# Softmax sums in one row of 512, added tile by tile, and query projections spread over more half steps

## The chip, the cores and the metric

The kernel runs on one core of a Trainium2 chip. A core has engines that work side by side, each through its own queue in order: PE (TensorE, matrix products and transposes), DVE (VectorE), ACT (ScalarE), POOL (GpSimd) and SP, which here only issues DMA transfers. The metric is the device time of one execution in microseconds (us); less is better. PE writes its results to PSUM, in banks of 128 partitions by 512 float32 numbers; the other engines read them from there.

## The reference

A decoder of two layers works on x of shape (4, 256, 256), that is four sequences b of 256 tokens. Layer 0 has self-attention, attention to a context of 1601 tokens, and a feed-forward part with ternary weights. Layer 1 has a gated recurrence, attention to the same context with projections, and a mixture of eight experts. The change touches the attention of layer 1, which is, cut to what matters:

```python
q = rms_norm((draft @ Wq.T).reshape(b, 256, 16, 128), q_norm_w)       # 16 query heads of 128
kv_in = concatenate([context, draft], axis=1)                         # 1857 keys
k = rms_norm((kv_in @ Wk.T).reshape(b, 1857, 4, 128), k_norm_w)       # 4 key heads
v = (kv_in @ Wv.T).reshape(b, 1857, 4, 128)
q, k = rope(q, draft_positions), rope(k, all_positions)
scores = einsum('bhqd,bhkd->bhqk', q, repeat(k, 4)) / sqrt(128)
attn = einsum('bhqk,bhkd->bhqd', softmax(scores), repeat(v, 4))
out = attn.reshape(b, 256, 2048) @ Wo.T
```

The softmax runs over the keys. The change alters how the sums of the exponentials, its denominators, are added up, and when the queries are projected.

## The kernel before

Layer 0 and the recurrence fill the first 450 us or so. Then comes a long stage of 32 *pairs*: for each b and each key head g (together a *head* in the code, 16 of them, list `heads`) two pairs of query heads. A pair (class `Pair`) has 512 columns, two query heads of 256 tokens, and 15 key chunks of 128 keys, handled as 8 tiles of two chunks (the last tile holds one chunk of 65 keys). Keys lie on partitions, queries along the row, so a tile is 128 x 2 x 512.

A pair passes through these methods:

- `score` (L1169): for each chunk PE makes the scores into a PSUM bank (bsc, L1181), ACT copies them with the factor of the keys (kn) into an s tile (L1182), and DVE keeps the running maximum (acc, L1184 and L1186). The s tiles come from a ring of 12 (`s_tile`, `NS`), so that the tile of step t is written again in step t + 12.
- `maximum` (L1188): PE transposes acc (tm), DVE reduces it, and PE spreads the maxima over a bank (bc, L1199).
- `exponential` (L1201): DVE subtracts bc from the s tile (L1203), ACT takes the exponential in place (L1206), and POOL adds the tile to `sum` (L1209 for tiles 0 and 1, L1211 for the rest). `sum` has 2 x 512 columns in one buffer.
- `weigh` (L1213): PE multiplies the values with the exponentials (bpo, L1220).
- `finish` (L1222): POOL adds the two halves of `sum` (L1225), ACT copies bpo out (aT, L1228), PE transposes the sum (ts, L1232), DVE reduces and inverts it (rs), PE spreads it (rb, L1239), DVE scales aT, and after the second pair of a head PE projects the result (bpw, L1247).

The next head is prepared meanwhile. `prep_q` (L1068 on; two calls a head, j = 0 and 1) projects 128 tokens onto four query heads (pq, L1078). In `rotate` ACT squares the result (L1033) and DVE makes two products (ropeq L1034, ropuq L1035). In `factor` POOL adds the halves of the rotation (L1040), DVE sums the squares (L1042), and POOL raises them to the power -1/2 (rnq, L1043). A half step or more later `normed` scales on ACT, four instructions (L1047), and later again PE transposes (tpq, L1090) and ACT copies out (L1091). `prep_kv` (L1097 on; four calls a head) does the same for up to four chunks of keys and values (pk L1115, ropek, ropuk, kn), with the key transposes tpk (L1124) and their copy kTb on ACT (L1126) as its second part. The weights of a head come by DMA on SP's queue (wq, wkv, wo, and context tiles cTk).

The order is written out by hand in `steps` (L1334): step s does the exponential of tile s - 10, the scores of tile s, then the other work of place 2s, the weighing of tile s - 11, then that of place 2s + 1. A place is thus half a step; a pair takes 16 places, a head 32. The loop from L1299 puts the parts of the next head at places: `QA` and `KA` give the steps of the projections of queries and keys after the head's base, `HB` the places from a query projection to its scaling, and `HC` those from a projection to its transposes, for queries and keys alike (L1318). Work that takes a PSUM bank gets a place of its own (`bank=True`): where the place is taken it moves to the next. A scheduler then fixes each engine's queue from this program, and may shift instructions a little where nothing depends on their order.

Short-lived results share six PSUM banks (`p1`): scores, pq, pk, all transposes but bc.

Of the kernel before, what the change touches and what calls it, by code (L numbers as in the profile page):

```python
# [10 lines left out]
F32 = mybir.dt.float32  # L11
# [5 lines left out]
ALU = mybir.AluOpType  # L17
# [3 lines left out]
P = 128  # L21
# [88 lines left out]
def decoder_kernel(ctx: ExitStack, tc: tile.TileContext, at, t, out):  # L110
    nc = tc.nc
    V, A, G, T = nc.vector, nc.scalar, nc.gpsimd, nc.tensor
# [6 lines left out]
    fr = ctx.enter_context(tc.tile_pool(name="fr", bufs=1))  # L119
# [11 lines left out]
    def p1(name):  # L131

        ring[0] += 1
        if psb and ring[0] % 3 == 0:
            return psb[0].tile([P, 512], F32, tag="one", name=name, bufs=2)
        return psa.tile([P, 512], F32, tag="one", name=name, bufs=4)
# [17 lines left out]
    def fa(b, name, dt=F32):  # L154

        return fr.tile([P, 512], dt, tag=f"a{b}", name=name, bufs=NA)
# [9 lines left out]
    def sm(shape, tag, name, bufs=2, dt=F32):  # L166
        return small.tile(shape, dt, tag=tag, name=name, bufs=bufs)
# [18 lines left out]
    def cc(name):  # L186
        o, n = at[name]
        return cst[:, o : o + n]

    ident = cc("ident")  # L190
# [969 lines left out]
    class Pair:  # L1160
# [40 lines left out]
        def exponential(self, c):  # L1201
            n, w, s = self.rows[c], self.wide[c], self.s[c]
            V.tensor_tensor(  # L1203
                s[0:n, 0:w, :], s[0:n, 0:w, :], self.bc[0:n, None, :].to_broadcast([n, w, 512]), ALU.subtract
            )
            A.activation(s[0:n, 0:w, :], s[0:n, 0:w, :], AF.Exp)  # L1206
            if c == 1:
                self.sum = fr.tile([P, 2, 512], F32, tag="sum", name=f"sum{self.nm}")
                G.tensor_tensor(self.sum, self.s[0], s, ALU.add)  # L1209
            elif c > 1:  # L1210
                G.tensor_tensor(self.sum[0:n, 0:w, :], self.sum[0:n, 0:w, :], s[0:n, 0:w, :], ALU.add)  # L1211

        def weigh(self, c):  # L1213
            e = gt[self.b, self.g]
# [7 lines left out]
        def finish(self):  # L1222
            b, g, nm = self.b, self.g, self.nm
            e, su = gt[b, g], self.sum
            G.tensor_tensor(su[:, 0, :], su[:, 0, :], su[:, 1, :], ALU.add)  # L1225
            aT = fa(1, f"aT{nm}")
            e[self.h] = aT
            A.copy(aT, self.po)  # L1228
            yield
            ts = p1(f"ts{nm}")  # L1230
            for i in range(4):
                T.transpose(ts[:, i * P : (i + 1) * P], su[:, 0, i * P : (i + 1) * P], ident)  # L1232
            rs = sm([P, 4], "rs", f"rs{nm}")
            V.tensor_reduce(rs, ts.rearrange("p (i k) -> p i k", i=4), AX.X, ALU.add)
            V.reciprocal(rs, rs)
            yield
            rb = p1(f"rb{nm}")
            for i in range(4):
                T.transpose(rb[:, i * P : (i + 1) * P], rs[:, i : i + 1].to_broadcast([P, P]), ident)  # L1239
            V.tensor_mul(aT, aT, rb)  # L1240
            yield
            if self.h == 2:
                pw = p1(f"bpw{b}{g}")
                for j in range(2):
                    for h in range(4):
                        o = (h % 2) * 256 + j * P
                        T.matmul(  # L1247
                            pw[:, j * 256 : j * 256 + 256], lhsT=e[h - h % 2][:, o : o + P], rhs=e["wo"][:, h, :],
                            start=h == 0, stop=h == 3,
                        )  # L1250
                xf = xs[b].rearrange("p j d -> p (j d)")
                V.tensor_add(xf, xf, pw)
# [6 lines left out]

    QA, KA, HB, HC = (3, 7), (11, 13, 15, 17), 4, 7
    DE, DW = 10, 11
    places, taken = {}, set()
    STEPS = NPAIR * len(pairs) + DW + 5
# [202 lines left out]
```

## Time and profile before

| what | value |
|---|---|
| median of 3 runs | 1853.54 us (1852.35 to 1856.31) |
| the profiled execution: its time, its span | 1854.56 us, 1852.8 us |
| granted TensorE clock, mean | 0.97 |
| PE busy | 1733.6 us (94%) |
| DVE, ACT, POOL busy | 1292.5, 1005.3, 834.9 us |
| POOL adds of exponentials (L1209, L1211, L1225) | 80.4, 424.1, 41.0 us |
| chain that ended last | PE 63%, DVE 11%, POOL 10%, ACT 10%, issue 4% |

The profile is one execution; its span runs from the first to the last instruction. Each line of a group names a source line, engine and operation, the result and the operands, their shape and the count, then busy time, the mean of one, and the time that the engine stood idle just before, with what ended that idleness after the arrow. A line of the waits reads: who, waited for whom: us in total, times, longest. A line of the timeline has the start, the duration, engine, line and operation; in brackets the idle time before it. Some PE records have 128x512 products in two pieces, so that two products count four.

### The profile page before, as it was taken

The page shows a single profiled execution, that of the slowest core. Times are in us where ns is not written, and L with a number is a line of the kernel's source. Part 1 is how long each engine was busy: PE and PEld are TensorE (multiplying, and loading weights), DVE is VectorE, ACT ScalarE, POOL GpSimd, SP SyncE. Part 2 cuts the span into 40 slices and gives each one's busy share as a digit, 9 for nine tenths or more (in the row PEclk, how much of TensorE's full clock was granted, in tenths as well). Part 3 has the DMA queues.
Part 4 walks back from the last instruction along what each step waited for, and adds up shares of the span by engine and source line. Part 5 has one row for each costly group of instructions (what it writes and reads, how often), then busy time and mean ns, then how long its engine had stood idle before and what let it go on. Part 6 is the DMA issues. An engine that isn't in the chain of part 4 may idle for free.

```text
span 1852.8 us, 19989 instructions
## 1 busy us (share of the span) xinstructions
PE 1733.6 (94%) x6576; PEld 1056.6 (57%) x6576; DVE 1292.5 (70%) x2396; ACT 1005.3 (54%) x1898; POOL 834.9 (45%) x524
## 2 busy tenths in 40 slices
PE   4779899989999999999999989999999999999997
PEld 3556786655555554655555555556565655556555
DVE  5785547787777668776767776676868676667754
ACT  1556536464656555665655565555646565455541
POOL 2100332111156565545656555655455566655470
PEclk8789899999999999999999999999999999999998
DMA  4010232001110110101011112101120111112000
GB/s 138 1 40 15 78 113 66 25 24 44 47 54 15 52 37 29 54 21 57 13 59 44 51 37 62 44 29 47 36 83 29 48 44 52 32 35 60 29 23 23
DMA packets 66214, 82.99 MB, mean 45 GB/s; under 512 B 6460, under 2 KB 49600, under 8 KB 66112
## 3 DMA queue, kind: packets, MB, share of 16 engines
q1 hardware_dynamic: 64960, 80.31, 14.2%
q10 hardware_dynamic: 1152, 1.41, 0.2%
q8 instruction: 53, 0.87, 0.2%
q14 instruction: 49, 0.40, 0.1%
HBM read 80.65 MB, written 1.05 MB: 44 GB/s over the span
## 4 chain that ended last, share of the span: by engine, by line
PE 63%; DVE 11%; POOL 10%; ACT 10%; issue 4%; DMA 0%; ACTq 0%; POOLq 0%; DVEq 0%
PE bpo L1220 14%; PE bsc L1181 14%; PE pk L1115 9%; POOL sum L1211 4%; POOL sum L1209 3%; PE bpw L1247 3%; ACT s L1182 3%; ACT s L1206 3%; DVE acc L1186 2%; PE mph L914 2%; PE xpo L607 2%; PE xsc L562 2%; PE pq L1078 1%; PE mpe L925 1%; ACT sm L463 1%
## 5 line engine op out<-in xcount | busy, mean ns | idle before, releaser
L1186 DVE SCALAR_TENSOR_TENSOR acc<-bsc,kn,acc 128x512 f32<-128x512 f32 x448 | 335.0, 748 | 215.9 <-ACT s L1182 205.2
L1181 PE MATMUL bsc<-qTb,kTb 128*128 128x512 f32 (+1 forms) x960 | 455.6, 594 | 5.7 <-DVE acc L1186 3.4
L1220 PE MATMUL bpo<-s,vb 128*128 128x512 f32 (+1 forms) x960 | 455.4, 595 | 1.1 <-ACT aT L1228 1.1
L1211 POOL TENSOR_TENSOR sum<-sum,s 128x1024 f32<-128x1024 f32 x192 | 424.1, 2209 | 16.5 <-ACT s L1206 2.4
L1182 ACT ACTIVATE s<-bsc,kn 128x512 f32<-128x512 f32 (+1 forms) x480 | 316.0, 687 | 184.8 <-PE bsc L1181 111.0
L1203 DVE TENSOR_TENSOR s<-s,bc 128x1024 f32<-128x1024 f32 (+1 forms) x256 | 288.7, 1144 | 13.7 <-PE bc L1199 13.7
L1206 ACT ACTIVATE s<-s 128x1024 f32<-128x1024 f32 (+1 forms) x256 | 254.4, 1013 | 61.2 <-DVE s L1203 59.9
L1220 PEld LDWEIGHTS bpo<-s,vb 128*128 128x128 f32 (+1 forms) x960 | 178.5, 191 | 166.6 <-issue 157.0
L1040 POOL TENSOR_TENSOR ropek<-ropek,ropuk 128x512 f32<-128x512 f32 (+1 forms) x64 | 76.8, 1200 | 402.2 <-DVE ropuk L1035 402.2
L1181 PEld LDWEIGHTS bsc<-qTb,kTb 128*128 128x128 f32 (+1 forms) x960 | 167.5, 187 | 150.4 <-issue 114.1
L1115 PE MATMUL pk<-wkv,cTk 128*128 128x256 f32 x832 | 194.4, 383 | 15.8 <-DVE acc L1186 15.8
L1115 PEld LDWEIGHTS pk<-wkv,cTk 128*128 128x128 f32 x832 | 157.7, 191 | 56.4 <-DVE acc L1186 21.3
L1040 POOL TENSOR_TENSOR ropeq<-ropeq,ropuq 128x512 f32<-128x512 f32 x32 | 41.0, 1282 | 173.0 <-DVE ropuq L1035 125.9
L1209 POOL TENSOR_TENSOR sum<-s,s 128x1024 f32<-128x1024 f32 x32 | 80.4, 2511 | 39.7 <-PE ts L1232 24.9
L1033 ACT ACTIVATE squares<-pk 128x256 f32<-128x256 f32 (+1 forms) x128 | 47.7, 375 | 90.4 <-PE pk L1115 80.8
L1047 ACT ACTIVATE ropeq<-ropeq,rnq 128x128 f32<-128x128 f32 x128 | 44.5, 396 | 91.0 <-POOL rnq L1043 91.0
L1034 DVE TENSOR_TENSOR ropek<-pk,ctabk 128x256 f32<-128x256 f32 (+1 forms) x128 | 52.0, 406 | 56.1 <-ACT squares L1033 55.9
L1118 ACT COPY vb<-pk 128x256 f32<-128x256 f32 (+1 forms) x128 | 46.1, 361 | 65.4 <-DVE ropuk L1035 62.7
L463 ACT ACTIVATE sm<-sc,mx 128x128 f32<-128x128 f32 (+1 forms) x128 | 52.2, 436 | 26.8 <-DVE mx L456 19.9
L1043 POOL TENSOR_TENSOR kn<-ssk,nhalf 128x4 f32<-128x4 f32 (+1 forms) x64 | 63.6, 994 | 0.0
L914 PE MATMUL mph<-yTm,wi 128*128 128x256 f32 x256 | 63.1, 392 | 0.0
L1126 ACT COPY kTb<-tpk 128x512 f32<-128x512 f32 (+1 forms) x64 | 35.2, 550 | 49.8 <-PE tpk L1124 49.8
(494 smaller groups left out, 2530.6 us busy)
## 6 DMA issues: line engine op xcount, KB each, us to landing
cTk<-in_ctxT SPq DMA_DIRECT2D x32, 512.0 KB, 3.8
wq<-in_wq SPq DMA_DIRECT2D x16, 512.0 KB, 4.9
wo<-in_wo SPq DMA_DIRECT2D x16, 512.0 KB, 3.8
wi<-in_wi SPq DMA_DIRECT2D x32, 256.0 KB, 2.9
xcT<-in_ctxT SPq DMA_DIRECT2D x12, 512.0 KB, 3.7
xct<-in_ctx SPq DMA_DIRECT2D x12, 512.0 KB, 3.6
cTk<-in_ctxT SPq DMA_DIRECT2D x16, 384.0 KB, 3.2
wkv<-in_wkv SPq DMA_DIRECT2D x16, 256.0 KB, 3.6
```

The lines of the kernel that those rows point to most:

```text
L463: A.activation(ex[:, h, k], scs[u][:, h, k], AF.Exp, bias=mx[:, j, i : i + 1], accum_out=sums[:, j, i : i + 1])
L914: T.matmul(ph[:, i * 256 : i * 256 + 256], lhsT=wi[:, i, c, f * ME : (f + 1) * ME], rhs=yT[:, c, :], start=c == 0, stop=c == 1,)
L1040: G.tensor_tensor(r4, r4, u4[:, :, ::-1, :], ALU.add)
L1115: T.matmul(pk[:, q, :], lhsT=src, rhs=e["wkv"][:, c, :], start=c == 0, stop=c == 1)
L1181: T.matmul(pc[0:n, :], lhsT=e["kT"][:, k * P : k * P + n], rhs=q, start=True, stop=True)
L1182: A.activation(s[0:n, i, :], pc[0:n, :], AF.Copy, scale=e["kn"][0:n, k : k + 1])
L1186: V.scalar_tensor_tensor(self.acc[0:n, :], pc[0:n, :], e["kn"][0:n, k : k + 1], self.acc[0:n, :], ALU.mult, ALU.max)
L1203: V.tensor_tensor(s[0:n, 0:w, :], s[0:n, 0:w, :], self.bc[0:n, None, :].to_broadcast([n, w, 512]), ALU.subtract)
L1206: A.activation(s[0:n, 0:w, :], s[0:n, 0:w, :], AF.Exp)
L1209: G.tensor_tensor(self.sum, self.s[0], s, ALU.add)
L1211: G.tensor_tensor(self.sum[0:n, 0:w, :], self.sum[0:n, 0:w, :], s[0:n, 0:w, :], ALU.add)
L1220: T.matmul(self.po, lhsT=e["v"][0:n, k, :], rhs=self.s[c][0:n, i, :], start=k == 0, stop=k == NCH - 1)
```

## The change

The sum of a pair becomes one row of 512 columns per partition, in two buffers that take turns between pairs. The first add comes with tile 0 and adds its two halves; each later tile is added half by half, two instructions for a tile of two chunks and one for the last. The add of the two halves at the end is dropped. The projections of queries move from steps 3 and 7 to steps 2 and 6 of the head before; the distance from projection to scaling grows from 4 to 5 places, that to the transposes from 7 to 8, for queries and keys.

```diff
@@ exponential
             A.activation(s[0:n, 0:w, :], s[0:n, 0:w, :], AF.Exp)
-            if c == 1:
-                self.sum = fr.tile([P, 2, 512], F32, tag="sum", name=f"sum{self.nm}")
-                G.tensor_tensor(self.sum, self.s[0], s, ALU.add)
-            elif c > 1:
-                G.tensor_tensor(self.sum[0:n, 0:w, :], self.sum[0:n, 0:w, :], s[0:n, 0:w, :], ALU.add)
+            if c == 0:
+                self.sum = fr.tile([P, 512], F32, tag="sum", name=f"sum{self.nm}", bufs=2)
+                G.tensor_tensor(self.sum, s[:, 0, :], s[:, 1, :], ALU.add)
+            else:
+                for i in range(w):
+                    G.tensor_tensor(self.sum[0:n, :], self.sum[0:n, :], s[0:n, i, :], ALU.add)
@@ finish
-            G.tensor_tensor(su[:, 0, :], su[:, 0, :], su[:, 1, :], ALU.add)
...
-                T.transpose(ts[:, i * P : (i + 1) * P], su[:, 0, i * P : (i + 1) * P], ident)
+                T.transpose(ts[:, i * P : (i + 1) * P], su[:, i * P : (i + 1) * P], ident)
@@ places
-    QA, KA, HB, HC = (3, 7), (11, 13, 15, 17), 4, 7
+    QA, KA, HB, HC = (2, 6), (11, 13, 15, 17), 5, 8
```

## The prediction

> **What bounds the kernel now.** I read the busy shares first, then the idle gaps of PE by what ended them, then the waits of the other engines, then the timeline around the repeated gaps.
>
> ```profile
> PE 1733.6 (94%) x6576; PEld 1056.6 (57%) x6576; DVE 1292.5 (70%) x2396; ACT 1005.3 (54%) x1898; POOL 834.9 (45%) x524
> ```
>
> PE is the bound. The table by stage gives 1320 us of PE work in the 1350 us from 450 to 1800, where the attention pairs run. Only idle PE time there can be won. The waits of PE in that stretch sum to 29.6 us; its three largest are:
>
> ```profile
> PE pk L1115 <- DVE acc L1186: 15.8, 13, 3.2
> PE mpe L925 <- DVE acc L1186: 3.8, 3, 1.3
> PE bsc L1181 <- DVE acc L1186: 3.4, 2, 2.8
> ```
>
> PE waits for a PSUM bank that the running maximum (acc) has yet to read. Why acc is late stands in the waits of all engines:
>
> ```profile
> DVE acc L1186 <- ACT s L1182: 205.2, 118, 5.8
> ACT ropeq L1047 <- POOL rnq L1043: 91.0, 25, 6.3
> ACT s L1182 <- POOL sum L1209: 62.3, 30, 5.5
> POOL sum L1209 <- PE ts L1232: 24.9, 5, 14.0
> ```
>
> acc waits for the score copy on ACT, and ACT waits on POOL: for the first add of a pair (L1209), which is the last reader of an s buffer that ACT wants to refill, and for the norm factors of the queries (rnq). The timeline shows one such case whole:
>
> ```profile
> 832.07 1.28 POOL L1040 TENSOR_TENSOR ropek<-ropek,ropuk 128x512 f32<-128x512 f32 x1 [14.29 <-DVE ropuk L1035]
> 833.30 1.03 POOL L1043 TENSOR_TENSOR kn<-ssk,nhalf 128x4 f32<-128x4 f32 x1
> 834.29 2.43 POOL L1209 TENSOR_TENSOR sum<-s,s 128x1024 f32<-128x1024 f32 x1
> 836.75 1.27 ACT L1182 ACTIVATE s<-bsc,kn 128x512 f32<-128x512 f32 x2 [2.01 <-POOL sum L1209]
> 837.48 0.75 DVE L1186 SCALAR_TENSOR_TENSOR acc<-bsc,kn,acc 128x512 f32<-128x512 f32 x1 [2.09 <-ACT s L1182]
> 838.28 0.48 PE L1115 MATMUL pk<-wkv,cTk 128*128 128x256 f32 x1 [2.40 <-DVE acc L1186]
> ```
>
> POOL stood idle for 14.29 us in front of the key rotation while finished exponentials lay waiting; the first add was queued behind it. The 2.40 us reach PE.
>
> I sort PE's gaps from 510 to 1780 (26.8 us) by what the chain shows before each. (A) First add behind a key rotation: 2.39, 2.40, 1.98, 1.99, 1.97 = 10.7. (B) First add behind a query rotation: 2.76, 0.95, 1.27, 1.26, 1.26 = 7.5. (C) The second query's factor behind the whole sum, and small rest: 8.6.
>
> [...]
>
> **The change part by part.** (1) The adds. Prices from the groups by form:
>
> ```profile
> L1211 POOL TENSOR_TENSOR sum<-sum,s 128x1024 f32<-128x1024 f32 x160 | 382.6, 2391 | 14.1 <-ACT s L1206 2.4
> L1209 POOL TENSOR_TENSOR sum<-s,s 128x1024 f32<-128x1024 f32 x32 | 80.4, 2511 | 39.7 <-PE ts L1232 24.9 <-ACT s L1206 14.9
> L1225 POOL TENSOR_TENSOR sum<-sum 128x512 f32<-128x512 f32 x32 | 41.0, 1280 | 2.5
> L1211 POOL TENSOR_TENSOR sum<-sum,s 65x512 f32<-65x512 f32 x32 | 41.5, 1296 | 2.4
> ```
>
> Before, a pair is 8 adds: 2.42 + 5 x 2.36 + 1.26 + 1.27 = 16.75 us at the medians, and 0.07 after each that the next one needs (the chain's "issue"): 17.3. After, it is 14 adds of 1.27: 18.7. So 1.4 us a pair, 45 us of POOL work more. [...] The 45 us lie beside PE, since POOL is idle 40% of most stages. The cover is missing only in the last pair, where POOL is the chain from 1788.65 to 1805.93. There the first add can start at the end of exponential 0 (1787.4) instead of 1: 1787.4 + 18.7 = 1806.1. Cost: +0.2.
>
> (2) The start of the sum. The first add needs one exponential instead of two, and writes the other sum buffer, so the 24.9 us of POOL waiting for the transposes (ts) fall away. The order of instructions on POOL changes with it: in the pair that starts a head, the first add and most often eight more now precede the key rotation; in the other pair, two or three precede the query rotation. Nothing then holds up the first release: A and B go, -18.2.
>
> (3) The query projections come two half steps earlier (QA), their scaling one (HB), their transposes one (HC). Each brings its wq load, square, two products, sum of squares, rotation and power along, unchanged in number. wq is issued one head ahead on SP's queue (489.65 for the matmul at 547.13) and keeps its place among the loads, so it can't be late. The second factor still follows the whole sum on POOL. The sum starts about 3 us sooner and takes 1.4 longer, so ACT's wait for it shrinks: I credit half of C, -4.3.
>
> (4) HC also serves the keys (KA), which do not move: their four transposes a head come a half step later, while the scores that read them stay. This is the costly part. I counted PE work between the last key transpose and the first score that reads it, in the order of instructions, at 0.86 us a 512-column matmul and 0.216 a 256-column one. Before: 6.1 to 7.0, 5.3 to 6.1, 5.3 to 6.1 and 4.0 to 4.9 us for the four groups. After: 1.0 to 1.4, 3.6, 1.8 to 2.7 and 2.3. In between ACT must copy the keys out (0.43 to 0.59). The trace of before shows how late that copy runs:
>
> ```profile
> 880.13 0.49 PE L1124 MATMUL tpk<-cst,ropek 128*128 128x128 f32 x3
> 881.69 1.27 ACT L1182 ACTIVATE s<-bsc,kn 128x512 f32<-128x512 f32 x2 [3.93 <-POOL sum L1209]
> 882.84 0.43 ACT L1126 COPY kTb<-tpk 128x321 f32<-128x321 f32 x1
> 899.69 0.69 ACT L1047 ACTIVATE ropeq<-ropeq,rnq 128x128 f32<-128x128 f32 x2 [4.06 <-POOL rnq L1043]
> ```
>
> The fourth copy ended 2.65 us after its transposes here, 2.1 to 4.3 over the heads; 2.0 are left after the change. What made it late, the first add, goes, but another wait comes: ACT's scaling of the first query now stands before that copy, and its factor follows three or four adds on POOL. Queued behind the scaling on ACT are two score copies for four times, three exponentials and the key copy; DVE waits for the score copies, PE for their banks and for the keys.
>
> I worked one head through from the start of its bc transposes with the durations above. Exponentials 0 to 2 end at 3.1, 4.7, 6.8; POOL adds to 8.7, rotates to 10.0, adds the other half of tile 2 to 11.2, and the factor is there at 12.2. ACT arrives at 8.5 and loses 3.7. Scaling, two exponentials and four score copies later the fourth key copy ends at 18.4. PE wants it at 16.7: 1.8 us lost. Eight of the 14 later heads have an add between rotation and factor, as this one. Where none is between (six heads) the factor is there at 9.8; four lose nothing and two about 0.85. Sum: 8 x 1.8 + 1.7 = +16.1. Bounds: 0, if ACT runs ahead once the first add no longer stops it, and 15 x 2.7 = 40, if every head loses the 1.8 and the third copy (1.8 us left, copies ended 1.1 to 2.5 late) about 0.9 more. I take 16 since both waits are worked from measured durations. The first group's 1.0 suffices as long as ACT is idle there, as before (it waited 0.8 to 1.9 us for tpk).
>
> Sum: -18.2 - 4.3 + 16.1 + 0.2 = -6.2. The profiled execution took 1854.56 (span 1852.8), 1.02 over the median of the runs: 1848.4, and 1847.4 as a median.
>
> **Rivals.** *Margins hold* (0.20): the new stalls stay under 0.3 us a head, so 22.5 less about 3: 1834. For it: the first factor of a head was waited for 1.7 to 3.2 us before in 8 heads, and in 7 not at all. Against: 2.0 us left where 2.1 to 4.3 were used. *Key copies decide* (0.31), the other side: ACT reaches the fourth, and the third, key copy late in all heads, 2.7 us a head: 40 - 22 = +18, 1871. It decides from 22.5/15 = 1.5 us a head on. For it: in-order ACT, shortened distances in all 15 heads. Against: PE that stalls gives ACT time, so stalls don't add up. *No effect* (0.09): the gaps only move, since PE is 98% full there: 1853.5. For it: 30 waits of 62.3 us for L1209 cost PE only 18. *Mine* (0.40), with its own range 1841 to 1854.
>
> **How the numbers follow.** A measurement tells 0.2% (3.7 us) from no change. Mine is 0.7 faster, 0.25 same, 0.05 slower; margins hold is faster; key copies slower; no effect same. Faster 0.28 + 0.20 = 0.48; same 0.10 + 0.08 = 0.18 (0.01 of no effect given to slower); slower 0.34. The range, with 1 in 10 outside each end, cuts half of "margins hold" and a third of "key copies": 1833 to 1871.
>
> **What would show it.** Right: no ACT wait for a first add and no POOL wait for ts; POOL about 880 us busy in 714 to 720 instructions; new PE or PEld waits of 1 to 2 us ended by kTb before the score matmuls, at most one or two a head; ACT waiting for rnq ahead of the fourth key copy. PE idle from 450 to 1800 near 24 us. Wrong: waits for kTb absent (then 1834), or over 1.5 us in every head (then 1871). A PE gap behind adds that now delay the key rotations would be a mechanism that I have not counted.

## The result, and the profile after

The changed kernel takes 1841.28 us (median of 6 runs, 1837.06 to 1841.77), the kernel before, on the same chip, 1853.36 us (6 runs, 1852.33 to 1856.31). The ratio is 0.9928, with a 95% interval of 0.9917 to 0.9938: 12.1 us faster, where 6 were forecast. The time lies inside the prediction's range, and just inside that of its likeliest case.

The busy time of the engines, from the page of the changed kernel:

```profile
PE 1727.6 (94%) x6576; PEld 1051.1 (57%) x6576; DVE 1288.4 (70%) x2396; ACT 1007.2 (55%) x1896; POOL 871.8 (47%) x716
```

The profiled execution took 1839.59 us, its span is 1837.7 us, 15.1 less than before. PE busy fell by 6.0 us (1733.6 to 1727.6), though the work on PE is the same, and the rest of the span, in which PE stands still, by 9.1 us (119.2 to 110.1). Both are needed for the sum; the prediction counted only the second kind. Nearly all of the gain lies between the first and the last score product (L1181), the *pair stage* from here on: 1300.3 us before and 1285.7 after, with 27.4 and 17.9 us of PE's idle time. What comes ahead of it, the same work in both, took 474.3 and 473.1 us, a difference of the size that these profiles show from one kernel to another (472.3 to 474.8 in all 14).

What PE waited for from 450 to 1800, the view in which the kernel before had "pk <- acc" with 15.8 us at its head:

```profile
PE bc L1199 <- DVE mq L1195: 5.5, 3, 2.5
PE rb L1239 <- DVE rs L1235: 4.6, 5, 1.0
PE tpk L1124 <- DVE it L921: 3.5, 5, 0.8
PE bsc L1181 <- ACT kTb L1126: 3.3, 7, 1.8
```

The gaps behind a first add are gone. The waits at bc and tpk are new; those for rs and kTb were 0.9 and 0.7 us before. PE's weight loads, which run beside its products, waited for kTb as well: 14.9 us in 27 places, 0.9 in one before. Among the waits of all engines the two that the change was to remove, ACT's for the first add (62.3 us before) and POOL's for the transposes ts (24.9), no longer appear. The two that matter for what follows read:

```profile
POOL sum L1209 <- ACT s L1206: 186.7, 32, 12.2
ACT ropeq L1047 <- POOL rnq L1043: 107.4, 32, 6.5
```

POOL now waits for the exponential in all 32 pairs, so the first add is no longer late. ACT's wait for the query factors grew from 91.0 to 107.4 us. This is a sum over both queries of a head, and they went opposite ways: the wait for the second factor shrank from 67.9 to 52.2 us, that for the first grew from 23.1 to 55.2. The timeline shows what a long one costs (start, duration, engine and line, operation, idle time before it and what ended it):

```profile
732.68 0.69 ACT L1047 ACTIVATE ropeq<-ropeq,rnq 128x128 f32<-128x128 f32 x2 [6.52 <-POOL rnq L1043]
733.28 0.67 ACT L1182 ACTIVATE s<-bsc,kn 128x512 f32<-128x512 f32 x1
733.98 0.75 DVE L1184 TENSOR_SCALAR acc<-bsc,kn 128x512 f32<-128x512 f32 x1 [5.88 <-ACT s L1182]
734.65 0.68 DVE L1195 TENSOR_REDUCE mq<-tm 128x4 f32<-128x512 f32 x1
735.38 0.65 PE L1199 MATMUL bc<-cst,mq 128*128 128x128 f32 x4 [2.49 <-DVE mq L1195]
```

ACT stands 6.52 us at the scaling of the second query. The first score copy of the next pair is queued behind it; DVE's first instruction of that pair (L1184) waits for that copy; and behind L1184 on DVE stands the reduction mq of the pair that has just ended, for which PE waits. The wait reaches PE only through what is queued behind it. It is one of the three longest, in the heads that open a new sequence, when DVE has rotation tables to make besides: there ACT waits 6.5, 6.5 and 4.9 us and PE, at bc, 2.49, 2.35 and 0.71. In all other heads ACT waits at most 3.5 us for the second factor and PE does not wait at bc.

The adds by form, the two kinds of 128 partitions (count, then busy time and mean ns of one, then the idle time before them):

```profile
L1212 POOL TENSOR_TENSOR sum<-sum,s 128x512 f32<-128x512 f32 x384 | 500.5, 1303 | 79.7 <-ACT s L1206 55.5
...
L1209 POOL TENSOR_TENSOR sum<-s 128x512 f32<-128x512 f32 x32 | 41.8, 1306 | 186.7 <-ACT s L1206 186.7
```

### The profile page after: what moved, and what is told of

Read it like the earlier page. It is cut to its first block, busy times and chain, and to the rows that moved or that the text cites. A ratio compares the mean times of both kernels' runs of the same rounds, so it can differ in the third digit from the quotient of the medians.

```text
span 1837.7 us, 20229 instructions
## 1 busy us (share of the span) xinstructions
PE 1727.6 (94%) x6576; PEld 1051.1 (57%) x6576; DVE 1288.4 (70%) x2396; ACT 1007.2 (55%) x1896; POOL 871.8 (47%) x716
## 4 chain that ended last, share of the span: by engine, by line
PE 72%; DVE 10%; ACT 8%; POOL 6%; issue 4%; POOLq 0%; DVEq 0%; ACTq 0%
PE bsc L1181 18%; PE bpo L1221 17%; PE pk L1115 11%; POOL sum L1212 3%; PE bpw L1247 3%; PE mph L914 2%; PE xpo L607 2%; ACT s L1206 2%; PE xsc L562 2%; ACT s L1182 2%; PE pq L1078 2%; PE mpe L925 1%; ACT sm L463 1%; PE pp L689 1%; PE tpk L1124 1%
## 5 line engine op out<-in xcount | busy, mean ns | idle before, releaser
L1212 POOL TENSOR_TENSOR sum<-sum,s 128x512 f32<-128x512 f32 (+1 forms) x416 | 541.0, 1301 | 81.9 <-ACT s L1206 55.5
L1181 PE MATMUL bsc<-qTb,kTb 128*128 128x512 f32 (+1 forms) x960 | 457.9, 597 | 3.3 <-ACT kTb L1126 3.3
L1181 PEld LDWEIGHTS bsc<-qTb,kTb 128*128 128x128 f32 (+1 forms) x960 | 172.1, 187 | 187.8 <-issue 145.8
L1221 PEld LDWEIGHTS bpo<-s,vb 128*128 128x128 f32 (+1 forms) x960 | 173.4, 191 | 141.3 <-issue 136.6
L1115 PE MATMUL pk<-wkv,cTk 128*128 128x256 f32 x832 | 190.1, 379 | 0.0
L1209 POOL TENSOR_TENSOR sum<-s 128x512 f32<-128x512 f32 x32 | 41.8, 1306 | 186.7 <-ACT s L1206 186.7
L1033 ACT ACTIVATE squares<-pk 128x256 f32<-128x256 f32 (+1 forms) x128 | 48.1, 377 | 96.3 <-PE pk L1115 74.7
L1047 ACT ACTIVATE ropeq<-ropeq,rnq 128x128 f32<-128x128 f32 x128 | 41.9, 390 | 107.4 <-POOL rnq L1043 107.4
L1184 DVE TENSOR_SCALAR acc<-bsc,kn 128x512 f32<-128x512 f32 x32 | 24.0, 749 | 83.5 <-ACT s L1182 83.5
L463 ACT ACTIVATE sm<-sc,mx 128x128 f32<-128x128 f32 (+1 forms) x128 | 52.2, 435 | 26.5 <-DVE mx L456 19.6
```

The source lines that it names most:

```text
L463: A.activation(ex[:, h, k], scs[u][:, h, k], AF.Exp, bias=mx[:, j, i : i + 1], accum_out=sums[:, j, i : i + 1])
L1115: T.matmul(pk[:, q, :], lhsT=src, rhs=e["wkv"][:, c, :], start=c == 0, stop=c == 1)
L1181: T.matmul(pc[0:n, :], lhsT=e["kT"][:, k * P : k * P + n], rhs=q, start=True, stop=True)
L1212: G.tensor_tensor(self.sum[0:n, :], self.sum[0:n, :], s[0:n, i, :], ALU.add)
L1221: T.matmul(self.po, lhsT=e["v"][0:n, k, :], rhs=self.s[c][0:n, i, :], start=k == 0, stop=k == NCH - 1)
```

## The experiments

Each was timed four times, beside seven runs of the kernel before on the same chip, 1 to 8 on one and 9 to 12 on another (medians of before 1852.5 to 1853.9). Kernel 6 leaves out all adds of a sum but the first. For each profile, the span split into PE's busy time and the rest:

| kernel | median us | ratio to before, 95% | span | PE busy | rest |
|---|---|---|---|---|---|
| before | 1853.4 | | 1852.8 | 1733.6 | 119.2 |
| changed | 1841.3 | 0.9917 to 0.9938 | 1837.7 | 1727.6 | 110.1 |
| 1 new sums, old places | 1882.2 | 1.0142 to 1.0172 | 1880.5 | 1745.1 | 135.4 |
| 2 old sums, new places | 1867.9 | 1.0064 to 1.0094 | 1867.0 | 1735.0 | 132.0 |
| 3 keys at 7 | 1828.6 | 0.9856 to 0.9886 | 1826.5 | 1722.5 | 104.0 |
| 4 one buffer | 1885.4 | 1.0158 to 1.0192 | 1883.3 | 1745.2 | 138.1 |
| 5 late start | 1840.8 | 0.9911 to 0.9945 | 1839.4 | 1730.6 | 108.8 |
| 6 first add only | 1812.1 | 0.9759 to 0.9788 | 1810.4 | 1717.1 | 93.3 |
| 7 keys at 6 | 1879.4 | 1.0126 to 1.0157 | 1876.5 | 1739.6 | 136.9 |
| 8 queries at 1, 5 | 1908.5 | 1.0271 to 1.0306 | 1907.1 | 1750.0 | 157.1 |
| 9 scaling ahead | 1864.1 | 1.0039 to 1.0069 | 1863.2 | 1736.9 | 126.3 |
| 10 keys at 6, scaling behind | 1832.1 | 0.9870 to 0.9900 | 1830.2 | 1725.3 | 104.9 |
| 11 first query only | 1830.9 | 0.9857 to 0.9890 | 1829.2 | 1730.1 | 99.1 |
| 12 last pair on DVE | 1823.8 | 0.9824 to 0.9854 | 1823.7 | 1723.1 | 100.6 |

### Each part alone, the keys, and the buffer (1 to 4)

My theory was that of the prediction: the sums bring about 18 us, and the places cost some 12, nearly all through the keys' shorter distance. The edits, each to the changed kernel:

```diff
# 1: the places of before
-    QA, KA, HB, HC = (2, 6), (11, 13, 15, 17), 5, 8
+    QA, KA, HB, HC = (3, 7), (11, 13, 15, 17), 4, 7
# 2: exponential and finish as before the change, the new places kept
# 3: the key transposes 7 places after the projection, those of queries 8
-                    put(spot + HC, gen, True, True)
+                    put(spot + (HC if f is prep_q else 7), gen, True, True)
# 4: one sum buffer
-                self.sum = fr.tile([P, 512], F32, tag="sum", name=f"sum{self.nm}", bufs=2)
+                self.sum = fr.tile([P, 512], F32, tag="sum", name=f"sum{self.nm}")
```

> The sums as after, the places as before. Theory (the first add gave the gain, the places give some back): the ACT waits for a first add and their PE gaps (10.7 + 7.5 us) go, no key copy is late; but in the queue order nine adds now stand before the first query's rotation in most heads, so its factor is late: 1838 to 1845 us, no PE wait for kTb. Rival (the places gave the gain, the sums nothing): 1850 to 1855 us, since the places are those of before.

> The places as after, the sums as before. Theory (first add): the five PE gaps behind a key rotation stay, since the first add still stands behind it on POOL, and the shorter way of the keys costs a few us more: 1850 to 1858 us. Rival (the places gave the gain): 1839 to 1845 us.

> As after, but the key transposes stay 7 places behind their projection. As predicted (late key copies cost 16 us): 1824 to 1830 us. By the trace of after (PE waits for kTb are 3.3 us; the other new waits are for the reciprocals and the maxima, behind ACT's wait for rnq): 1836 to 1841 us, with the waits for rs and mq still there.

> As after, but the sum has one buffer, so that the first add of a pair waits for the transposes (ts) of the pair before. Theory (the second buffer is half of the early start): POOL waits for ts come back, 20 us or more, ACT waits for a first add come back, 1845 to 1853 us. Rival (the early first add alone suffices): 1839 to 1843 us.

Kernel 3 came out near the prediction's price: the keys' distance costs 12.7 us (1841.3 to 1828.6), with the queue order that comes with it. In the changed kernel POOL has a further add between the first query's rotation and its factor in 9 of the 16 heads, in kernel 3 in none, and ACT's wait for that factor is 44.4 us there in place of 55.2. The other three missed. Each part alone is a loss, 29.7 and 15.4 us against the kernel before on the same chip (1852.5), and together they gain 12: the parts don't add up, and a sum of prices cannot give the result. In kernel 1, PE waits for the keys in a way that the keys' distance, which is the old one there, does not explain:

```profile
PE bsc L1181 <- ACT kTb L1126: 24.4, 10, 3.6
```

The timeline of kernel 1 before one of these waits:

```profile
717.67 5.34 POOL L1212 TENSOR_TENSOR sum<-sum,s 128x512 f32<-128x512 f32 x4 [0.15 <-ACT s L1206]
...
722.97 2.18 POOL L1040 TENSOR_TENSOR ropeq<-ropeq,ropuq 128x512 f32<-128x512 f32 x1
727.07 1.28 ACT L1047 ACTIVATE ropeq<-ropeq,rnq 128x128 f32<-128x128 f32 x4 [6.60 <-POOL rnq L1043]
728.25 0.41 ACT L1126 COPY kTb<-tpk 128x321 f32<-128x321 f32 x1
728.71 3.78 PE L1181 MATMUL bsc<-qTb,kTb 128*128 128x512 f32 x4 [3.33 <-ACT kTb L1126]
```

The first query's rotation is queued behind the adds on POOL; in most heads nine of them stand before it in the queue's order, in this one seven (one at L1209 and six at L1212). DVE had finished its part at 720.68 (L1042, from 720.01, 0.67 long). The factor comes late, ACT stands at the scaling, and the fourth key copy is queued behind the scaling. ACT's waits for the first factor sum to 93.8 us in this kernel, those for the second to 31.8.

In kernel 4 the first query's rotation goes ahead of the whole sum again, and the first add waits for the transposes of the pair before it, as it did before the change:

```profile
POOL sum L1209 <- PE ts L1232: 53.4, 14, 13.5
...
PE bc L1199 <- DVE mq L1195: 31.9, 14, 3.7
```

The whole sum then runs late, the second query's factor behind it too, and PE pays at bc. The second buffer, with the queue order that it allows, is worth 44.1 us with these places. Kernel 2, with the old sums in their one buffer, shows the same two waits, 55.4 us of POOL for ts (14 times) and 10.5 of PE for mq (8 times).

### What the sum's parts are worth (5 and 6), and other distances (7 and 8)

```diff
# 5: the sum starts with tile 1
-            if c == 0:
+            if c == 1:
...
-                G.tensor_tensor(self.sum, s[:, 0, :], s[:, 1, :], ALU.add)
-            else:
+                G.tensor_tensor(self.sum, self.s[0][:, 0, :], self.s[0][:, 1, :], ALU.add)
+            if c > 0:
# 6: kernel 1 without the adds of tiles 1 to 7
-            else:
-                for i in range(w):
-                    G.tensor_tensor(self.sum[0:n, :], self.sum[0:n, :], s[0:n, i, :], ALU.add)
# 7: as 3, with 6 in place of 7
# 8: as 3, and
-    QA, KA, HB, HC = (2, 6), (11, 13, 15, 17), 5, 8
+    QA, KA, HB, HC = (1, 5), (11, 13, 15, 17), 6, 9
```

> The changed kernel, but the sum starts with tile 1, as before the change: its first add (the halves of tile 0) is issued after the second exponential, and the halves of tile 1 follow. Same number of adds, two sum buffers, same places, and the order on POOL's queue stays nearly that of the changed kernel. It tells the early start from the second buffer. Theory (the second buffer carries the gain, since one buffer cost 44 us and made POOL wait 53 us for the transposes ts; the start itself is worth only the time between two exponentials, some 1.6 us, on an engine with slack): 1840 to 1846 us, PE waits within 4 us of those after the change. Rival (the early release of the first s buffer is what removed the PE gaps): ACT's waits for the first add return above 30 us, PE gaps behind acc return, 1850 to 1860 us.

> The new sums with the places of before (1882 us), and of each pair's sum only the first add is kept: the other adds are left out of the computation, so POOL has about 13 adds of 1.3 us fewer a pair, while the places on PE, ACT and DVE stay. Theory (new sums alone lose because the first query rotation and factor stand behind up to nine adds on POOL, so ACT stands at the scaling and brings the key copies late): PE's waits for kTb fall from 30 us to under 6, the waits of ACT for rnq from 125 us to under 40, the clock returns to 0.97, and the time falls to 1830 to 1842 us (30 us of waits, about 14 of clock, and 3 of the tail less). Rival (the places of before don't fit for a reason on PE or ACT, such as the order of PE's instructions; the adds are only beside it): 1865 to 1880 us, with kTb waits above 15 us.

> The changed kernel with the key transposes 6 places after the projection (8 in the changed kernel: 1841 us; 7: 1828.6 us). Theory (the transposes only need to be so early that no score waits for kTb, and at 7 only 1.1 us of such waits are left): 1826 to 1832 us, no further gain, kTb waits of PE under 2 us. Rival (every place that the keys come earlier gives some 12 us, by relieving ACT and DVE too): 1812 to 1820 us.

> Keys at 7 places, and the query projections one step earlier still (steps 1 and 5, scaling 6 places later, transposes 9), so that the scaling stays in its place and the first query's rotation and factor stand ahead of the sum on POOL in nearly all heads. Theory (what is left after the keys are put back is ACT's wait for query factors, 103 us in all, which makes the running maximum late): the waits for rnq fall under 70 us and the time to 1818 to 1826 us. Rival (the first add, now behind the query rotation, frees the s buffer late, as in the kernel before): ACT waits for the sum of over 30 us, 1832 to 1845 us. If neither matters: 1827 to 1831 us.

Kernel 5 equals the changed kernel (1840.8 to 1841.3), and POOL's queue has the adds in the same places between the rotations and factors: starting the sum one exponential earlier is worth nothing that can be measured. Kernel 6 falls by 70 us against kernel 1, more than the 40 to 52 expected. In the pair stage it is 62.3 us: 39.6 of idle time and 20.5 from a clock that no longer drops there (its mean over the whole span is 0.959 in kernel 1 and 0.974 in kernel 6; see the last section); 6.2 are the end, where nothing waits for the last adds any more. PE's wait for kTb falls from 24.4 us to 0.7, ACT's for rnq from 125.2 to 50.0 (under 40 was expected). So the adds on POOL were the cause in kernel 1, and the places suited PE and ACT. Kernel 6 takes away all adds but one; that those ahead of the first factor did the harm is for kernel 11 to show.

Kernels 7 and 8 missed by some 50 and 80 us, on the slow side, and broke a theory of mine: that earlier keys are harmless once none is waited for, and that the factor has to come early for the first query. Both show one new wait, PE for the running maximum at its transposes:

```profile
PE tm L1193 <- DVE acc L1186: 28.1, 14, 4.9
```

This is kernel 7; kernel 8 has 48.4 us in 15 waits. Comparing the order of the instructions on ACT's queue with that of kernel 3, I found one difference that could do it: the scaling of the second query stands ahead of the last score copy of its pair (65 x 512) in 11 of the 16 heads of kernel 7, and in 15 of kernel 8, there most often ahead of the last two; in kernel 3 and in the changed kernel it stands behind that copy in all.

### What stands behind a waiting scaling (9 to 12)

Kernel 9 has the keys of kernel 3 and the order of 7; kernel 10 has the keys of 7 and the order of 3.

```diff
# 9: as 3, and
-    QA, KA, HB, HC = (2, 6), (11, 13, 15, 17), 5, 8
+    QA, KA, HB, HC = (2, 6), (11, 13, 15, 17), 6, 9
# 10: as 7, and
-    QA, KA, HB, HC = (2, 6), (11, 13, 15, 17), 5, 8
+    QA, KA, HB, HC = (2, 7), (11, 13, 15, 17), 5, 8
# 11: of the places of before only the first query moves
-    QA, KA, HB, HC = (2, 6), (11, 13, 15, 17), 5, 8
+    QA, KA, HB, HC = (2, 7), (11, 13, 15, 17), 4, 7
# 12: as 11, and in the last pair
+                E = V if c >= 4 and (self.b, self.g, self.h) == (B - 1, NKV - 1, 2) else G
                 for i in range(w):
-                    G.tensor_tensor(...)
+                    E.tensor_tensor(...)
```

> Keys at 7 places, query projections at steps 2 and 6 as in the changed kernel (1828.6 us with scaling 5 and transposes 8 places later); here scaling 6 and transposes 9 places later. The order on POOL's queue stays; on ACT's queue the scaling of the second query comes to stand ahead of the last score copy of the pair (65x512) instead of behind it. Theory (a wait of ACT for a query factor costs only through what is queued behind it: ahead of the last score copy it holds up the running maximum and PE's transposes tm of it): PE waits for acc at tm in about 14 pairs, 2 to 3 us each, and some clock: 1868 to 1882 us, as with the keys at 6 places, which had the same order. Rival (the keys at 6 places were themselves what cost 50 us): 1826 to 1834 us.

> Keys at 6 places, which took 1879 us, but the second query's projection one step later (steps 2 and 7 instead of 2 and 6), so that its scaling stands behind the last score copy on ACT, among the score copies of the next pair. Theory (order on ACT): PE's waits for acc at tm vanish, 1822 to 1834 us. Rival (keys at 6 places cost by themselves, for example by tpk taking ACT and PSUM at a bad moment): 1865 us or more.

> The new sums with all places of before, but the first query projection of a head one step earlier (steps 2 and 7 instead of 3 and 7; scaling 4 and transposes 7 places later). The least change of places that puts the first query's rotation behind three adds instead of nine. Theory (that queue on POOL was the whole trouble of the new sums with the old places, 1882 us): 1824 to 1832 us, PE's waits for kTb under 3 us. Rival (the second query has to move too): 1840 us or more.

> The kernel with the first query projection alone moved, and in the very last pair the adds of tiles 4 to 6 (five of 14) are done by DVE, which has little to do there, instead of POOL. With the keys at 7 places PE waited 3.7 us at the end for the last add of POOL, and one add of 1.34 us on POOL should take about 0.7 us on DVE (its subtraction of 512 columns takes 0.67 us). Theory (the tail is bound by POOL's last adds): 2 to 5 us less than with the same places and all adds on POOL. Rival (the end of the output products hides them): within 1 us.

Kernels 9 and 10 point the same way. Kernel 9, with the scaling ahead of the last copy in the same 11 heads as in kernel 7, is 35.5 us slower than kernel 3 (1864.1; I had expected 4 us more at least). Kernel 10, with the keys at 6 and the scaling behind that copy, takes 1832.1, 47 us less than kernel 7. The order on ACT costs most of what kernel 7 lost. PE's waits at tm are 22.3 us in kernel 9 and 1.6 in kernel 10, 28.1 in kernel 7 and 2.3 in kernel 3. The keys at 6 places cost 3.5 us at most, near the noise, with the scaling behind (kernels 10 and 3), but 15.3 with it ahead (7 and 9), which is not explained. Kernel 9 also has the query transposes a place later; PE never waits at them in its trace. The timeline of kernel 9:

```profile
820.71 0.69 ACT L1047 ACTIVATE ropeq<-ropeq,rnq 128x128 f32<-128x128 f32 x2 [6.53 <-POOL rnq L1043]
821.31 0.67 ACT L1182 ACTIVATE s<-bsc,kn 65x512 f32<-65x512 f32 x1
822.01 0.75 DVE L1186 SCALAR_TENSOR_TENSOR acc<-bsc,kn,acc 65x512 f32<-65x512 f32 x1 [8.05 <-ACT s L1182]
822.81 0.86 PE L1193 MATMUL tm<-cst,acc 128*128 128x128 f32 x4 [4.96 <-DVE acc L1186]
```

And the like place in kernel 3:

```profile
880.35 0.68 ACT L1182 ACTIVATE s<-bsc,kn 65x512 f32<-65x512 f32 x1 [0.34 <-PE bsc L1181]
...
883.94 0.60 PE L1193 MATMUL tm<-cst,acc 128*128 128x128 f32 x4
884.68 1.28 ACT L1047 ACTIVATE ropeq<-ropeq,rnq 128x128 f32<-128x128 f32 x4 [3.18 <-POOL rnq L1043]
```

In kernel 9 the copy of the 65 keys comes after the wait and PE stands 4.96 us; in kernel 3 it is out before, and the transposes tm run while ACT still waits for the factor. In total ACT waits nearly alike in both, 107.6 us in kernel 9 and 102.9 in kernel 3, with 35 us between their times.

Kernel 11 shows how little of the new places is needed: with the new sums, moving the first query projection of each head by one step turns 1882.2 into 1830.9. Its factor then follows three or four adds in place of seven or nine, and ACT's waits for it fall from 93.8 to 43.9 us, though all adds are done and the fourth key copy stands behind the scaling as before. The second query need not move, and HC stays at 7. The kernel differs from kernel 3 by less than the intervals tell. One or two score copies of the next pair stand ahead of the second query's scaling here, none in most heads of kernel 3, and PE's waits at bc (4.7 us there) do not occur.

At its end kernel 11 keeps one wait for the sum, the last add of the last pair:

```profile
PE ts L1232 <- POOL sum L1212: 4.0, 1, 4.0
```

Kernel 12 takes 7.1 us off, more than expected. The expectation says five adds of tiles 4 to 6; it was tiles 4 to 7, seven adds (POOL's instructions fall from 716 to 709), at 0.69 us on DVE. Between the profiles it is 5.5 us, and it lies after the last score product (80.5 us in kernel 11, 74.7 in 12): 4.8 us are busy time of PE and only 1.1 idle time, since PE waits 2.8 us for an exponential instead. (Over the whole span the idle time is 1.5 us longer, through the stage ahead of the pairs, where the work is the same.) After the wait of 4.04 us that ended at 1780.43 the granted clock in kernel 11 was 0.50 and 0.59 in the next two stretches of 5 us; in kernel 12 at this point (1780 to 1790) 1.00 and 0.92. At 1823.8 us it is the fastest here that computes the whole sums, 30.0 us below the 1853.8 of the kernel before in the same comparison.

## Why the prediction was right or wrong

**The first-add gaps (-18.2).** Right: A and B are gone, with the two waits named. The reason was half right. Of the two things that step (2) credited, the second buffer carries it (one buffer: 44.1 us slower), with the order on POOL that comes with it; the earlier start carries nothing (kernel 5). And the saving holds only with a moved first query: kernel 1 has the new sums too, and PE stood still 16.2 us longer in it than before the change.

**The adds.** Right: 716 instructions, 871.8 us of POOL where some 880 were forecast, 1.30 us each on the mean where 1.27 were taken. They are hidden only as far as no query factor stands behind them; "the 45 us lie beside PE" was too simple. At the end of the last pair PE waited 3.2 us for them, 2.5 before: +0.7 for the +0.2 of the forecast.

**The query moves (-4.3, as half of C).** The credit came in part: ACT's wait for the second factor shrank from 67.9 to 52.2 us, and what PE pays behind it is 5.5 us at bc, where C, with its small rest, was 8.6. But the moves didn't earn it. With the new sums and the old places that wait is 31.8 us (kernel 1), with the first query alone moved 32.5 (kernel 11), so moving the second lengthens it. The step failed in what it left out: what the first query's move is worth. The prediction saw that few adds precede that query's rotation after the change (two or three by its count, three or four in the trace), but took this as the state of things, not as the work of the new places. With the old places it is nine in most heads, and the first query's move alone is worth 51.3 us (1882.2 to 1830.9, kernels 1 and 11).

**The key transposes (+16.1).** Near in size: undoing the shorter distance gave 12.7 us. The wait that was foreseen is there: ACT stands at the first query's scaling, ahead of the fourth key copy, for 2.4 to 4.1 us in each of the 14 later heads; 3.7 were worked out for eight of them, and the other six were put lower. PE's loss behind it was only in part as told. PE waits for kTb 3.3 us, not 16, and its weight loads 14.9. From the changed kernel to kernel 3 the pair stage is 11.2 us shorter: 7.7 of it is idle time of PE, where the waits for rs (4.6), for it (3.5) and for kTb go or shrink, and 3.6 busy time. The clock is no part of this, since both profiles have one stretch of half clock in that stage, after gaps of 2.49 and 2.31 us; what shortened the busy time is open. That the late key copy spread over what DVE and ACT had queued behind it would fit these waits, but no run took the two apart.

**What was missing from the sum.** The busy time of PE. In the pair stage it fell by 5.0 us, and 3.4 of these I put down to the clock: it dropped to one half for 3.41 us three times before the change and once after, and half of that, 1.7 us, is my estimate for each. The sum counted gaps at their own length only. So the -6.2 of the forecast stand against -14.6 in the pair stage: -9.5 of idle time and -5.0 of busy time. That the median fell into the likeliest case's range, by 0.3 us, is in part luck: the first-add saving hung on a move that was not credited, the key copies cost less than forecast, and the clock was left out. The forecast of PE's waits from 450 to 1800, near 24 us, was met by chance too: 22.9 after 29.6, with other causes in the list, and 4.0 of the 22.9 belong to the end of the last pair, which before the change lay behind 1800. The rival "margins hold" (1834) named the right side for a wrong reason: the margins did not hold.

**Size of the loss side.** The rival "key copies decide" (1871) did not come about, but kernels 1, 2, 4, 7, 8 and 9 all lie between 1864 and 1909. One place more or less for one kind of work turned a gain into such a loss; the prediction's idea of stalls that stay within 3 us a head was too narrow for the neighbours of this change.

## What to carry to other kernels

On engines that work in order, ask of each instruction that waits what stands behind it, not how long it waits: 103 and 108 us of the same wait went with times 35 us apart. An edit that makes a helper engine's work longer or earlier is to be judged with the queue order that it produces, and parts that decide that order together can't be priced one by one. A second buffer may be worth much where an earlier start is worth nothing.

## What the runs showed of the hardware

Some of PE's waits cost more than their length here. In the 14 kernels, from 450 to 1775 us, I compared PE's gaps of 1.6 us or more with the granted clock in the 5 us after each. Of 25 gaps up to 2.05 us one was followed by half clock, of 42 from 2.06 to 3.1 us 23, of 24 above 3.1 us 23. In the first trace the gaps of 2.76, 2.40 and 3.19 us were followed by it, with a mean of 0.66 over the 5 us, the one of 2.39 was not (1.00). The one of 2.49 us shown above was (0.66), and the two score products after it (four records) took 3.45 us instead of 1.88. Each of these four stretches of half clock, three before the change and one after, lasted 3.41 us. In kernel 1, after the gap of 3.33 us shown above, the clock was 0.50 in each of the five stretches of 1 us from 729.01 to 734.01. The length of a gap alone does not tell whether half clock follows: 2.40 and 2.39 us went opposite ways in the first trace, 2.88 and 2.87 in kernel 1. What else decides is not shown by these counts.

Two of POOL's instructions in the timeline of kernel 1 were long as well: the rotation at 722.97 took 2.18 us and the power after it 1.93, while DVE made a table of 960 columns (from 722.60 to 726.16); the medians of the 32 are 1.27 and 1.02. Two of the 32 query rotations in kernel 1 ran over 1.3 times their median and two of the powers, so this is a small part of the late factors there.
